# First quad's layer 0: one product or seven, and the order of what surrounds it

## The chip, the cores and the metric

The kernel runs on one core of a Trainium2 chip. The metric is the device time of one execution in microseconds (us); the median of the runs is compared. Engines are called by the profile's names where rows are read: PE is TensorE, PEld its weight loads, DVE is VectorE, ACT is ScalarE, POOL is GpSimd, SP is the queue of SyncE that issues most transfers.

## The reference

Sixteen batches of 1024 nodes with 128 features pass two layers over one 1024x1024 weighted adjacency matrix. All is float32.

```python
# layer 0
h = relu(layernorm(x))
x = x + adj @ (h @ W) + b
# layer 1: five gated steps
h = relu(layernorm(x))
for _ in range(5):
    m = adj @ h                                   # m_in and m_out are the same: one adj
    u = h @ U3.T + bu3
    z = sigmoid([m, m] @ W3.T + b3 + u)
    r = sigmoid([m, m] @ W4.T + b4 + u)
    hv = tanh([m, m] @ W5.T + b5 + (r * h) @ U5.T + bu5)
    h = (1 - z) * h + z * hv
out = x + h
```

## The kernel before

The batches are worked on in four quads of four. `adj @ h` (the aggregation) is the bulk of the work. A full two-level aggregation (`aggregate`, its matmuls are L502 of the profile) splits the adjacency matrix and the states into 2x2 blocks twice, and multiplies by seven products instead of eight at each level: 49 small products of two 128x128x256 matmuls each. It needs sums of the blocks on both sides. The sums of adjacency blocks ("right sums") are made once and stored to HBM (`rd`), from where they stream through a ring of 14 slots in SBUF; some are kept resident. The sums of states ("left sums") are made on VectorE in every aggregation (`big`, `little`). The opening of the program has to do, beside layer 0 of the first two quads, all that makes this possible.

The opening runs in this order. Quad 0's layer 0 is an aggregation without any trick (`aggregate_plainly`): for each half g of the nodes and each batch, eight matmuls of 128x128x512 over eight chunks c of the nodes, 64 in all. Quad 1's is `aggregate_by_seven`: one level of the seven products, each with four matmuls for i = 0 and four for i = 1 (two batches share a block row), 56 in all. Its right operands are the adjacency quarters R11, R21, R22 (raw tiles as loaded) and four sums T1 to T4 of quarters; its left operands are halves of the normed batches and four sums S1 to S4. Product p of `BIG = (1, 2, 6, 5, 7, 3, 4)` takes R11, R21, T2, T1, T3, R22, T4 in that order. T1 to T4 lie in ring slots, so the ring can be filled only when the products that read them are done. After each matmul group comes ScalarE's copy out of PSUM or VectorE's add from PSUM into the result tile `mT`. `po` multiplies a half of `mT` by the layer-0 weights (four 128x128x128 matmuls) and VectorE adds it to x (`xt`). Then follow layer 1's norm (`b0` to `b7`), and for quad 0 a store of the states in 32x32 squares (`park`, ft tiles), a load back (`sqt`) and VectorE's transposes of 32x32 squares (`transposing`, L699) that give the states with features on partitions.

The order is written out by hand. `pin` keeps program order on each engine, `put(k, piece)` hangs a piece of work behind place k, and `place(k)`, called after each product of an aggregation, emits what hangs there. So each engine runs its queue strictly in the written order, and an instruction that waits holds up all that stands behind it on its engine. Gate places have names such as "Az0" (pair A, second stage, first unit).

A layer norm is a `Norm`: `statistics` (VectorE, one `bn_stats` per chunk, L330), `scales` (VectorE aggregates and adds epsilon into `ve`, L339 and L341; POOL takes the inverse root `rstd`, L342), `shift` (VectorE's `nmr`, L347, which waits for POOL), `relu` (ScalarE, one activation per chunk, L360).

Loads are gated by tiny VectorE memsets: a memset of one element of the target tile makes the transfer wait until VectorE has come to that place. Before, all loads go out on SP in three such groups; x of batch 0 comes in three parts, adjacency tiles `raw[i][g]` (i: quarter rows, g: column half) in 512 KB pieces.

Step 0 of quad 0 is the first two-level aggregation, with quad 1's layer-1 norms beside it. Its left sums for the next products, the norm's statistics and the adds into the results all run on VectorE. After its 49 products come the gates. All later steps are the same in both kernels.

Of the kernel before, what the change touches and what calls it, by code (L numbers as in the profile page):

```python
# [96 lines left out]
def tile_two_gnn_layers(  # L97
# [50 lines left out]
    for n in (HALF, HALF, BLK):  # L148
        pin(nc.tensor.matmul(unread[:, 0:n], zeros[:, 0:P], zeros[:, 0:n], start=True, stop=True))
# [26 lines left out]
    def load_adj(i, g):  # L176
        parts = SB if (i, g) == (0, 0) else 1
        for k in range(parts):
            cs = bass.ts(k, SB // parts)
            dma(raw[i][g][:, cs], adjT[:, bass.ts(i, SB), bass.ts(g, HALF)][:, cs])  # L180

    xts = {0: load_x(0, parts=((0, 2), (2, CH), (CH, NC)))}
    xts.update({b: x_tile(b) for b in range(1, Q)})
    for i in range(2):
        load_adj(i, 0)

    early_x = {}

    def other_loads(k):
        if k == 0:
            pin(nc.vector.memset(xts[1][:, 0, 0:1], 0.0))
            load_x(1, xts[1])
            load_adj(2, 0)
        elif k == 1:
            pin(nc.vector.memset(raw[3][0][:, 0, 0:1], 0.0))
            load_adj(3, 0)
        else:
            pin(nc.vector.memset(xts[2][:, 0, 0:1], 0.0))  # L200
            for b in range(2, Q):
                load_x(b, xts[b])
            for i in range(NB):
                load_adj(i, 1)
            for b in range(Q, Q + 3):
                early(b)
            dma(gb, gbias.to_broadcast([P, D]))
            dma(w_sb, weights)
            dma(b_sb, biases)
# [31 lines left out]
    def right_sums():  # L241

        rooms = [flat(ring[:, 4 * k : 4 * k + 4]) for k in range(3)]
        count = [0]

        def big_sum(n):
            room = rooms[{1: 2, 2: 0, 3: 1, 4: 2}[n]]
            T[n] = [room[:, bass.ts(k, N)].rearrange("p (c n) -> p c n", c=SB) for k in range(2)]
            for k in range(2):
                R = {(a, b): raw[2 * (a - 1) + k][b - 1] for a in (1, 2) for b in (1, 2)}  # L250
                a, b = {
                    1: (R[1, 2], R[1, 1]),
                    2: (R[2, 2], T.get(1, [0, 0])[k]),
                    3: (R[2, 2], R[1, 2]),
                    4: (R[2, 1], T.get(2, [0, 0])[k]),
                }[n]
                sub(T[n][k], a, b)
# [10 lines left out]
        def small_sums(i, part):  # L268
# [3 lines left out]
            if part == 0:  # L272
                for p, block in ((1, r[1, 1]), (2, r[2, 1]), (3, r[2, 2])):
                    store_right((i, p), block)
# [12 lines left out]
        steps = [lambda n=n: big_sum(n) for n in (1, 2, 3)]  # L287
        steps += [lambda i=i, h=h: small_sums(i, h) for i in (3, 2, 0, 4, 1, 5) for h in range(2)]
        steps += [lambda: big_sum(4)]
        steps += [lambda h=h: small_sums(6, h) for h in range(2)]  # L290
        return steps
# [249 lines left out]
    def aggregate_plainly(hN, nm, place):  # L541

        k = 0
        for g in range(NH):
            for i in range(Q):
                bank = ps_g.tile([P, HALF], F32, tag="pg", name=f"pq_{nm}_{i}_{g}")
                for c in range(NC):
                    pin(
                        nc.tensor.matmul(
                            bank,  # L550
                            hN[i][:, c, :],
                            raw[c // SB][g][:, c % SB],
                            start=c == 0,
                            stop=c == NC - 1,
                        )
                    )
                    if c == CH - 1:
                        k += 1
                        place(k)
                pin(nc.scalar.copy(mT[:, i, bass.ts(g, HALF)], bank))  # L560
                k += 1
                place(k)

    def aggregate_by_seven(hN, nm, place):

        S = {}
        for n in (2, 1, 3):
            t = flip.tile([P, 2, CH, D], F32, tag="sq", name=f"S{n}_{nm}")
            S[n] = [t[:, i] for i in range(2)]
        S[4] = []  # L570
        for i in range(2):
            t = work.tile([P, HALF], F32, tag="hv", name=f"S4{i}_{nm}", bufs=3)
            S[4].append(t.rearrange("p (j d) -> p j d", j=CH))

# [3 lines left out]
        def left_sums(n):  # L578
            for i in range(2):
                op, x, y = {  # L580
                    1: (add, part(1, 0, i), part(1, 1, i)),
                    2: (sub, S[1][i], part(0, 0, i)),
                    3: (sub, part(0, 0, i), part(1, 0, i)),
                    4: (sub, part(0, 1, i), S[2][i]),
                }[n]
                op(S[n][i], x, y)
# [4 lines left out]
        left_sums(1)  # L591
        left_sums(2)
        banks, fifth = {}, {}
        k = 0
        for p in BIG:
            right = big_right(BIG.index(p)) if p in (1, 2, 3) else T[{5: 1, 6: 2, 7: 3, 4: 4}[p]]
            for i in range(2):
# [9 lines left out]
                name = {2: "b", 5: "c", 3: "c"}.get(p, "a")  # L607
# [5 lines left out]
                elif p == 5:  # L613
                    banks[name, i] = ps_g.tile([P, HALF], F32, tag="pg", name=f"{name}{i}_{nm}")
                bank = banks[name, i]
                for c in range(CH):
# [5 lines left out]
                            start=p in (1, 2, 5) and c == 0,  # L622
# [4 lines left out]
                if p == 2:  # L627
                    add(result(0, 0, i), bank, result(0, 0, i))
                elif p == 3:
                    add(result(0, 1, i), bank, result(0, 1, i))  # L630
                elif p == 5:
                    fifth[i] = work.tile([P, HALF], F32, tag="z", name=f"P5{i}_{nm}")
                    pin(nc.scalar.copy(fifth[i], bank))
                else:
                    o = {1: result(0, 0, i), 6: result(0, 1, i), 7: result(1, 1, i), 4: result(1, 0, i)}[p]
                    pin(nc.scalar.copy(o, bank))
                    if p == 7:
                        add(o, o, fifth[i])
                k += 1
                if k in (3, 4):  # L640
                    left_sums(k)
                place(k)

# [93 lines left out]
    def po(b, g):  # L737
# [12 lines left out]
        add(half, pt, half)  # L750
# [387 lines left out]
    one, two = Norm(xts[0], firsts[0][1], "a0"), Norm(xts[1], firsts[1][1], "a1")  # L1138
    parts = (range(2), range(2, CH), range(CH, NC))
    for k in range(2):  # L1140
        one.statistics(parts[k])
        one.scales(parts[k])
        if k == 0:
            other_loads(0)
    one.shift(parts[0])
    one.relu(parts[0])
    one.statistics(parts[2])
    one.scales(parts[2])
    other_loads(1)
    one.shift(parts[1])  # L1150
    one.relu(parts[1])
    one.shift(parts[2])
    one.relu(parts[2])
    two.statistics(range(CH))
    other_loads(2)
    two.statistics(range(CH, NC))
    two.scales(EVERY)
    two.shift(EVERY)
    two.relu(EVERY)
# [3 lines left out]
    def sums_at(k, n):  # L1163
        for _ in range(n):
            put(k, sums.pop(0))

    def norm_at(k, src, dst, nm, done=None, now=None):

        box = {}

        def begin():
            box["n"] = Norm(src(), dst, nm)
            box["n"].statistics(EVERY)
            box["n"].scales(EVERY)

        def rest():
            box["n"].shift(EVERY)
            box["n"].relu(EVERY)
            if done:
                done()  # L1180

        put(k, begin)
        if now is not None:
            sums_at(k, now)
        put(k + 1 if now is None else k, rest)

    norm_at(1, lambda: xts[2], firsts[2][1], "a2")
    norm_at(2, lambda: xts[3], firsts[3][1], "a3", now=0)
    sums_at(3, 1)
    for b, k in zip(range(Q, 2 * Q), (4, 5, 6, 8)):  # L1190
        done = (lambda: early(2 * Q - 1)) if b == Q else None
        norm_at(k, lambda b=b: early_x[b], seconds[b - Q][1], f"a{b}", done, 1)
    for b in range(Q):
        put(8 + b, lambda b=b: bias(b))
    for k in (7, *range(9, 16)):
        sums_at(k, 1)
    for b in range(Q):
        put(11 + b, lambda b=b: po(b, 0))
    put(15, lambda: po(0, 1))
    put(16, lambda: po(1, 1))  # L1200
    aggregate_plainly([s for s, _ in firsts], "a0", place)

    put(1, lambda: po(2, 1))
    put(2, lambda: po(3, 1))
# [6 lines left out]
    for (load, turn), k in zip(turns, (7, 8, 11, 12)):  # L1211
        put(k, load)
    for b in range(Q):
        norm_at(2 * b + 1, lambda b=b: xts[b], nat[:, b], f"b{b}", lambda b=b: first_done(b))
        put((3, 5, 7, 10)[b], lambda b=b: xts.update({Q + b: load_x(Q + b)}))
        put((6, 8, 10, 14)[b], lambda b=b: bias(Q + b))
    for k in (2, 4, 8, 9, 10):
# [81 lines left out]
```

## Time and profile before

| what | value |
|---|---|
| median of 3 runs | 1771.12 us (1770.43 to 1771.25) |
| the profiled execution | 1769.81 us, of which the span from first to last instruction is 1767.9 us |
| granted clock of TensorE | 1.00 in every stretch |
| first product of quad 0 | 5.90 us |
| first product of quad 1's layer 0 | 69.85 us |
| first product of step 0 | 126.85 us |
| first gate of step 0 | 170.08 us |

Times in the views are microseconds from the start of the span. A row of the order in time gives start, length, engine, line, operation, output and inputs, shapes, the number of instructions merged in it, and in brackets the idle time before it with what ended that. Every float32 matmul shows as two instructions, and the length of a row includes the drain of the last one, so the pitch is the distance between the starts of rows.

### The profile page before, as it was taken

What the parts mean: (1) busy time and instruction counts of PE and PEld (TensorE: products, weight loads), DVE (VectorE), ACT (ScalarE), POOL (GpSimd) and SP (SyncE); (2) the same over time, 40 slices, a digit from 0 to 9 for tenths busy, and PEclk for the clock granted to TensorE, in tenths of its full rate; (3) what the DMA queues carried; (4) which work ended last, traced back from release to release, by engine and by line L of the source; (5) the groups of instructions that cost most, each with busy time, mean ns of one, the idle gap of its engine ahead of it and who ended that gap; (6) DMA issues with size and microseconds to landing.
All of it is one profiled execution on the core that took longest, in us unless ns stands there. A gap on an engine that the chain in (4) does not pass through costs nothing.

```text
span 1767.9 us, 21431 instructions
## 1 busy us (share of the span) xinstructions
PE 1759.5 (100%) x6436; PEld 1201.0 (68%) x6436; DVE 1374.9 (78%) x2807; ACT 899.1 (51%) x1976; POOL 58.9 (3%) x41
## 2 busy tenths in 40 slices
PE   9999999999999999999999999999999999999999
PEld 4557667588585766858857667585766858667584
DVE  6778889777878687887687968777687777868687
ACT  5246555544555555554456554545455454545545
POOL 3101000000000000000000000000000000000000
PEclk9999999999999999999999999999999999999999
DMA  7499776678495956749749577594866749476684
GB/s 255 156 322 316 227 261 209 184 238 250 131 303 181 290 191 198 237 137 287 235 143 329 176 224 282 158 289 158 256 202 203 249 133 293 165 232 223 200 283 175
DMA packets 170258, 396.88 MB, mean 224 GB/s; under 512 B 18592, under 2 KB 88096, under 8 KB 170144
## 3 DMA queue, kind: packets, MB, share of 16 engines
q1 hardware_dynamic: 169712, 395.00, 69.6%
q8 instruction: 52, 0.85, 0.2%
q14 instruction: 62, 0.51, 0.1%
q10 hardware_dynamic: 432, 0.52, 0.1%
HBM read 314.44 MB, written 81.00 MB: 224 GB/s over the span
## 4 chain that ended last, share of the span: by engine, by line
PE 95%; DVE 2%; POOL 1%; DMA 1%; ACT 0%; issue 0%; DVEq 0%; POOLq 0%
PE a L502 27%; PE c L502 13%; PE b L502 7%; PE a_a L502 3%; PE pr_3B L806 2%; PE pr_2B L806 2%; PE pr_1B L806 2%; PE pr_0B L806 2%; PE pr_3A L806 2%; PE pr_2A L806 2%; PE pr_1A L806 2%; PE pr_0A L806 2%; PE pr_4B L806 2%; PE pr_4A L806 2%; PE a_a L618 2%; PE pv_1B L806 2%
## 5 line engine op out<-in xcount | busy, mean ns | idle before, releaser
L502 PE MATMUL a<-ring,big 128*128 128x256 f32 x1120 | 287.9, 379 | 0.3 <-ACT Z L521 0.3
L521 ACT COPY Z<-a 128x256 f32<-128x256 f32 x480 | 177.0, 371 | 193.0 <-PE a L502 192.9
L239 DVE TENSOR_TENSOR Z<-Z,taps 128x512 f32<-128x512 f32 (+1 forms) x264 | 144.6, 554 | 165.3 <-ACT taps L521 165.0
L502 PE MATMUL c<-ring,little 128*128 128x256 f32 x960 | 246.4, 379 | 0.0
L502 PEld LDWEIGHTS a<-ring,big 128*128 128x128 f32 x1120 | 212.2, 190 | 37.5 <-issue 8.1
L239 DVE TENSOR_TENSOR mT<-mT,Z 128x1024 f32<-128x1024 f32 x154 | 188.4, 1223 | 22.9 <-ACT Z L521 17.3
L502 PEld LDWEIGHTS c<-ring,little 128*128 128x128 f32 x960 | 182.2, 190 | 25.1 <-ACT taps L521 0.2
L521 ACT COPY taps<-c 128x256 f32<-128x256 f32 x280 | 103.6, 370 | 115.8 <-PE c L502 110.6
L502 PE MATMUL a<-resident,little 128*128 128x256 f32 x560 | 143.8, 379 | 0.0
L502 PE MATMUL b<-ring,big 128*128 128x256 f32 x560 | 143.7, 379 | 0.0
L502 PE MATMUL a<-ring,little 128*128 128x256 f32 x560 | 143.7, 379 | 0.0
L502 PEld LDWEIGHTS a<-resident,little 128*128 128x128 f32 x560 | 106.3, 190 | 14.7 <-ACT Z L521 0.3
L502 PEld LDWEIGHTS a<-ring,little 128*128 128x128 f32 x560 | 106.4, 190 | 14.5
L502 PEld LDWEIGHTS b<-ring,big 128*128 128x128 f32 x560 | 106.4, 190 | 14.5
L667 DVE STREAM_TRANSPOSE sq<-hT_all 128x512 f32<-128x512 f32 x152 | 98.6, 686 | 0.0
L239 DVE TENSOR_TENSOR little<-big 128x256 f32<-128x256 f32 x154 | 64.2, 417 | 21.5 <-ACT big L399 21.3
L399 ACT COPY big<-nat 128x512 f32<-128x512 f32 x132 | 80.7, 614 | 0.0
L521 ACT COPY taps<-b 128x256 f32<-128x256 f32 x140 | 52.0, 371 | 55.7 <-PE b L502 54.8
L236 DVE TENSOR_TENSOR little<-little,big 128x256 f32<-128x256 f32 x154 | 65.5, 425 | 6.7
L236 DVE TENSOR_TENSOR little<-big 128x256 f32<-128x256 f32 x154 | 64.4, 418 | 0.0
L236 DVE TENSOR_TENSOR little<-big,little 128x256 f32<-128x256 f32 x154 | 64.3, 418 | 0.0
L521 ACT COPY mT<-a 128x256 f32<-128x256 f32 x80 | 29.8, 372 | 48.3 <-PE a L502 48.3
(287 smaller groups left out, 2913.1 us busy)
## 6 DMA issues: line engine op xcount, KB each, us to landing
ring<-rd SPq DMA_DIRECT2D x440, 512.0 KB, 5.9
fn<-sq SPq DMA_DIRECT2D x76, 512.0 KB, 3.8
nat<-fn SPq DMA_DIRECT2D x256, 128.0 KB, 5.6
x1d<-xt SPq DMA_DIRECT2D x16, 512.0 KB, 5.2
sqt<-ft SPq DMA_DIRECT2D x16, 512.0 KB, 6.9
xt<-x1d SPq DMA_DIRECT2D x16, 512.0 KB, 7.4
xt<-in_x_dram SPq DMA_DIRECT2D x15, 512.0 KB, 5.5
ft<-hb SPq DMA_DIRECT2D x48, 128.0 KB, 5.2
```

Source lines behind the costliest of these rows:

```text
L236: pin(nc.vector.tensor_sub(o, a, b))
L239: pin(nc.vector.tensor_add(o, a, b))
L399: return [lambda i=i: pin(nc.scalar.copy(made_of(k, i), part(a, b, i))) for i in range(2)]
L502: nc.tensor.matmul(bank, l, right[:, c, :], start=opens and c == 0, stop=c == SB - 1, skip_group_check=True,)
L521: pin(nc.scalar.copy(to, bank))
L618: nc.tensor.matmul(bank, left[:, c, :], right[c // SB][:, c % SB], start=p in (1, 2, 5) and c == 0, stop=c == CH - 1, skip_group_check=True,)
L667: pin(nc.vector.transpose(squares_of_half(sq, g), transposed_half(hT, g)))
L806: nc.tensor.matmul(bank, w_sb[:, w, :], moving, start=start, stop=stop, skip_group_check=True)
```

## The change

Quad 0's layer 0 is done by `aggregate_by_seven` too, in the order (1, 2, 3, 5, 6, 7, 4), and `aggregate_plainly` is gone. Since product 3 now comes before product 5, it gets a PSUM bank of its own (`apart`, bank "d"), is copied out, and product 6's bank is added to it. The left sums S1 to S4 of quad 0 live in the state tile `hT_all[:, 0]`, which step 0 fills later; half of T4 lives there too.

Around it: the warm-up multiplication on zeros loses its third, narrower matmul. Loads come in four gated groups: the first half of x of batches 0 and 1 on SP with the first two adjacency tiles issued by ScalarE's queue; then the second halves and tile 2; then tile 3 and the batches 2 and 3; then the other adjacency halves; then the rest. The norms of the first quad run by half batches, the statistics of one half ahead of the `shift` of the half before it. The stores of plain adjacency blocks become pieces of their own (`store_blocks`), and VectorE's work in the opening is re-ordered: right sums, big sums in halves, delayed adds (`late`), `po` in two parts so that its add comes one place later (`po_at`). The layer-0 bias is no longer added on VectorE: ScalarE fills `xt` with the bias, and a load issued by POOL accumulates x into it (`with_bias`). Quad 0's transposes (their `sqt` loads on SP and VectorE's instructions) move from quad 1's layer 0 into step 0, at the places 15, 26, 49 and "Az0"; the weight sums move into step 0, place 5. The ring's first loads are issued inside quad 1's layer 0 (places 11 to 14). The relus of quad 1's layer-1 norms come one per place rather than two.

```diff
-    for n in (HALF, HALF, BLK):
+    for n in (HALF, HALF):
         pin(nc.tensor.matmul(unread[:, 0:n], zeros[:, 0:P], zeros[:, 0:n], start=True, stop=True))
...
+    xts = {b: x_tile(b) for b in range(Q)}
+    load_x(0, xts[0], ((0, 1), (1, 2), (2, CH)))
+    pin(nc.vector.memset(raw[0][0][:, 0, 0:1], 0.0))
+    load_adj(0, 0, nc.scalar)
+    load_x(1, xts[1], ((0, CH),))
+    load_adj(1, 0, nc.scalar)
...
     def other_loads(k):
         if k == 0:
+            mark(xts[0][:, CH, 0:1])
+            for b in range(2):
+                load_x(b, xts[b], ((CH, NC),))
             load_adj(2, 0)
         elif k == 1:
+            mark(raw[3][0][:, 0, 0:1])
             load_adj(3, 0)
+            for b in range(2, Q):
+                load_x(b, xts[b], ((0, CH), (CH, NC)))
+        elif k == 2:
+            mark(raw[2][1][:, 0, 0:1])
+            for i in (2, 3, 0, 1):
+                load_adj(i, 1)
         else:
+            mark(gb[:, 0:1])
+            dma(gb, gbias.to_broadcast([P, D]))
             for b in range(Q, Q + 3):
                 early(b)
...
+    def with_bias(b):
+        if b not in xts:
+            xts[b] = x_tile(b)
+        both = gb.unsqueeze(1).to_broadcast([P, NC, D])
+        pin(nc.scalar.copy(xts[b], both))
+        pin(nc.gpsimd.dma_start(out=xts[b], in_=by_slots(x[b]), accum_op=ALU.add))
...
-    aggregate_plainly([s for s, _ in firsts], "a0", place)
+    late = {(2, 0): 5, (2, 1): 5, (6, 0): 10, (6, 1): 10}
+    aggregate_by_seven([s for s, _ in firsts], S, "a0", place, (1, 2, 3, 5, 6, 7, 4), late)
...
+    for (load, turn), begun, done in zip(turns, (8, 17, 40, 46), (15, 26, 49, "Az0")):
+        put(begun, load)
+        put(done, turn)
...
-        for n in range(CH):
-            put(9 * k + 11 + n, lambda b=b, n=n: h1[b].relu(range(2 * n, 2 * n + 2)))
+        for n in range(NC):
+            put(9 * k + 10 + n, lambda b=b, n=n: h1[b].relu(range(n, n + 1)))
...
+    put(5, weight_sums)
     step(0, (41, 43, "Ar0", "Ar2"), early_places)
```

## The prediction

> **What bounds the kernel now.** I read the page first, then TensorE's waits, the stretches up to the first layer-1 gates, and the order of time there. The page:
>
> ```profile
> span 1767.9 us, 21431 instructions
> PE 1759.5 (100%) x6436; PEld 1201.0 (68%) x6436; DVE 1374.9 (78%) x2807; ACT 899.1 (51%) x1976; POOL 58.9 (3%) x41
> ...
> PE 95%; DVE 2%; POOL 1%; DMA 1%; ACT 0%; issue 0%; DVEq 0%; POOLq 0%
> ```
>
> TensorE (PE) is busy for 1759.5 of 1767.9 us and carries the chain. All that it ever waited for:
>
> ```profile
> PE unread L149 <- DVE zeros L146: 1.5, 1, 1.5
> PE po L741 <- DVE xt L239: 0.9, 1, 0.9
> PE pq_a L549 <- ACT nat L360: 0.7, 2, 0.4
> PE pq_a L549 <- DMA big<-in_adjT_dram: 0.7, 1, 0.7
> PE pf L932 <- DVE hT_all L239: 0.4, 1, 0.4
> PE a L502 <- ACT Z L521: 0.3, 1, 0.3
> ```
>
> So only fewer matmuls shorten this kernel, and a matmul saved counts only as far as no new wait stands in its place. The stretches (columns: from:to, length, busy us of PE, PEld, DVE, ACT, POOL, clock, DMA share, GB/s) are quad 0 before its first `po`, its rest, quad 1's layer 0, and step 0 up to its gates:
>
> ```profile
> 0.00:46.17 46.17, 43.30 (x95) 18.55 (x96) 31.52 (x163) 25.66 (x61) 15.82 (x15) 1.00 0.71 248
> 46.17:69.85 23.68, 22.78 (x89) 12.87 (x88) 16.58 (x24) 5.41 (x12) 0.57 (x1) 1.00 0.61 221
> 69.85:126.85 57.00, 57.00 (x194) 30.22 (x193) 41.86 (x127) 20.32 (x46) 6.63 (x4) 1.00 0.72 246
> 126.85:170.08 43.23, 42.96 (x199) 36.83 (x198) 38.67 (x128) 29.17 (x82) 6.87 (x4) 1.00 0.93 315
> ```
>
> VectorE has room until 126.85 and little after it (38.67 of 43.23). The rates come from the order of time (start, length, count; every fp32 matmul is two instructions):
>
> ```profile
> 1.45 4.64 PE L149 MATMUL unread<-zeros 128*128 128x512 f32 x6 [1.45 <-DVE zeros L146]
> 5.90 1.32 PE L549 MATMUL pq_a<-big,nat 128*128 128x512 f32 x2
> ...
> 78.51 7.03 PE L618 MATMUL b_a<-big,hT_all 128*128 128x512 f32 x16
> 85.38 7.03 PE L618 MATMUL a_a<-ring,S_a 128*128 128x512 f32 x16
> ```
>
> From 78.51 to 85.38 eight matmuls take 6.87 us: 0.859 each. A `po` of four narrow ones takes 0.89 (46.17 to 47.06). These and later numbers without a fence are rows of the same view.
>
> **The matmuls removed.** Quad 0 drops from 64 to 56 (the order of instructions confirms it): 8 x 0.859 = 6.87 us. Before, step 0 begins at 126.85 = 120 x 0.859 + 16 `po` x 0.89 (117.32) + 9.53 of start and stalls. After, the work is 110.44; the question is what stands in place of the 9.53. I walk the new order with these rows.
>
> **The start.** The first 64 KB of x land near 2.85 (128 KB did at 2.95). Statistics, aggregate, `ve`, `rstd`, `nmr` and relu for one chunk end at 4.85 (two chunks: 2.98 to 5.87 before). The warm-up loses two half-width instructions, and the first adjacency part comes from ACT's queue, issued while SP issues x; first product 5.05 (was 5.90). Chunk 1 follows at 6.0; chunk 2 waits for the second adjacency tile: 1.57 MB from 1.9 us at 258 to 292 GB/s (the 2 to 8 us rows) gives 8.0. Batch 1's half is normed from 9.3. Product 1 ends near 13.25: 1.33 of waits. The row of the zeros shows about 0.8 us per 512-wide instruction against 0.43 later, so the engine starts slow. The Trainium skill ("TensorE: Matmul & The Clock Gate", Part 1) says that about 3.4 us of sustained work are needed to open the clock, and that an idle gap as long closes it; a shorter warm-up speaks against the change, and by that rule alone a missed window would cost up to 1.7 us (an estimate; 1764.7 in the end). I book nothing, as product 1 is fed late anyway.
>
> **Products 2 and 3.** Product 2 (second halves, adjacency tiles 2 and 3) needs 2.62 to 3.14 MB, there by 12.8, and batch 1's second half, whose `nmr` stands on VectorE behind batch 2's statistics (landing 13.5, read by 14.8): relu from 15.1 against 16.7 needed, no wait; it ends at 20.1. Product 3 needs sums over all four batches, 4.19 MB of loads (15.6). A half batch costs VectorE 1.37 (5.08 to 6.36 in the trace, and an `nmr`), hence `nmr` of batch 3's halves at 19.2 and 20.9. The left sums are 128x256 steps of 0.42 at a pitch under 0.4 (the `little` rows), three per quarter: 20.6 and 22.1 for i=0; for i=1, behind the 1.15 us half of T1, 24.55 and 25.6. TensorE waits 0.5 before each i; product 3 ends at 28.0.
>
> **Products 5, 6, 7, 4.** Product 5 needs T1 (26.75): covered. After it VectorE runs T2 (to 29.05), two PSUM adds (30.3), batch 4's statistics (`ve` at 32.5), and then waits for POOL:
>
> ```profile
> 21.74 0.17 DVE L341 TENSOR_SCALAR ve_a<-mv_a 128x8 f32<-128x8 f32 x1
> 22.08 1.64 POOL L342 TENSOR_TENSOR rstd_a<-ve_a,mhalf 128x8 f32<-128x8 f32 x1 [2.67 <-ACT nat L360]
> 33.79 2.45 POOL L342 TENSOR_TENSOR rstd_a<-ve_a,mhalf 128x8 f32<-128x8 f32 x1 [2.67 <-DVE ve_a L341]
> ```
>
> The root takes 1.64 us alone and up to 2.45 beside VectorE sums. `nmr` at 34.75, batch 5's statistics and T3 to 40.0, product 6's add 40.8, the `po` add, half of T4, batch 6's statistics 44.8, `nmr` 47.1, and the add that completes result (0,1) at 47.75. `po(0,1)` stands on TensorE right after product 7's first half, at 46.9: it waits 0.85. Later adds are ahead of need (T4's second half 49.4 against 54.7). Quad 1 begins at 61.7 instead of 69.85. Its VectorE work, about 48 us by the same durations, lies under 57 of TensorE; its third and fourth left sums are done near 82 and 91 against 91 and 98, its residual sums and stores near 99, and six of the seven ring loads are issued there rather than from 115.33. So no wait: step 0 begins at 110.44 + 5.05 + 1.33 + 1.0 + 0.85 = 118.67, **8.2 us earlier**.
>
> **The bias.** Eight VectorE adds of 1.22 (9.8 us) go; eight ACT copies of 128x1024 (twice a 0.56 copy: 1.1) and eight accumulating loads on POOL come, four SP loads of x go. ACT does the first four from 24.3 to 28.7, ahead of copies that product 6's add needs only at 40; POOL issues the first at 25.4, and behind the four stands batch 4's `rstd`, wanted at 32.8. With t us of POOL per load, it is late by 25.4 + 4t - 32.8. The trace has no such load. The nearest POOL rows are 1.64 (late by nothing) and 2.45 (2.4 us late, passed on to `po(0,1)`); a gain beyond 0 is excluded, as TensorE doesn't wait for the old adds. I take 1.64, a row without contention, and keep 2.4 for the range. Landing is no issue by the plain loads (4 to 10.7 us; 15 are allowed). The skill's "SBUF — State Buffer" (two separate sides) warns of descriptors that GpSimd cannot write while VectorE holds the shared port: 0.62 us became 3.1. By that, 4t = 12.4 makes `rstd` 5.0 late, and the gain an estimated 3.2.
>
> **Step 0.** Moved in: four transposes (each a 512 KB load on SP and two 0.65 us VectorE instructions) and the weight sums (1.1 us). Before, one transpose of 1.29 already lay inside, with 1.25 of left sums that are now done earlier: net VectorE load 38.67 + 1.1 + 1.1 (third transpose, at the end) = about 41 of 43. The fourth lies in the gates, where VectorE is busy 6 of 10 us. On SP the first load stands behind three ring loads and goes out 5.7 us into the step, landing 6.9 later (the page's `sqt` median) at 12.6; VectorE reaches the transpose at 14.4. The left sums stay ahead of their products by 0.45 us at the tightest (fourth sum of the fourth big product) and 0.8 to 1.9 elsewhere. Before, step 0 lost 0.9 (43.23 against 49 x 0.864), after ScalarE ran relus in pairs between copies; they come singly now. I leave 0.9; bounds 0 and 2.4 (0.9 and a transpose's 1.29 unhidden, rounded up).
>
> Beyond, the order of instructions is the same, so the gain passes through: 1769.81 (this execution: 1767.9 span and 1.9 around it) - 8.2 = 1761.6. The median 1771.12 lies 1.3 above this execution: **1763.0**, rounded.
>
> **The rivals.** *Loads feed the norms late.* If the opening loads keep the first 6 us' 265 GB/s instead of reaching 350 to 400, batch 2 lands 1.7 us later, and products 3 and after slip by that: 1764.7. For it: smaller descriptors at the start. Against: 8 to 12 us already ran at 350 to 367.
> *VectorE falls behind* in step 0 and at `po(0,1)`: +1.5 and +2.4 (POOL at 2.45): 1766.9. For it: margins under 1 us in order; against: 10 us of its work is gone.
> *Slower: the accumulating loads hold POOL.* At t = 3.9 the lateness is 8.2 and the gain is gone; from t = 4.8 (11.8 late) the kernel is slower by over 0.2%; at t = 6 it is 16.6 late, 1779.6. Place: batch 4's `rstd`, in front of every VectorE step that product 7 needs. For it: no accumulating load in the trace. Against: POOL's longest instruction is 2.45.
> *The change isn't what it says*: excluded by the order, 56 matmuls and not 64.
>
> **How the numbers follow.** 0.2% (3.5 us) is about what a measurement of this kernel can tell from no change. Forecast 0.62; loads late 0.13; VectorE behind 0.13; POOL 0.12, two thirds of it past t = 4.8. Faster by over 0.2% (below 1767.6): 0.62 + 0.13 + over half of VectorE's case = 0.83; slower: 0.08; within: the rest, 0.09. The range: below, the waits of 1.0 and 0.85 and step 0's 0.9 not appearing, 1760.2; above, VectorE's case with the late loads (1.7), 1768.6.
>
> **What would show it.** Right: `aggregate_by_seven` starts near 5.05; TensorE waits of about 0.5 on the left sums near 20 and 24 and 0.85 at a `po` near 47; quad 1 at 61.7; step 0 at 118.7; gates 43 later; PE busy down by some 7. Wrong: a VectorE wait on POOL over 3 us near 33, waits on adjacency or x loads beyond 14 us, step 0 over 44.5, or steps after it that differ.

## The result, and the profile after

The changed kernel takes 1775.64 us (median of 8 runs, 1773.92 to 1777.46); the kernel before took 1771.11 beside it (8 runs, 1769.55 to 1772.91). The ratio is 1.0027, with a 95% interval of 1.0016 to 1.0038: slower by about 0.27%, where 8 us less were forecast. The execution profiled took 1773.92 us, the fastest of the eight, so what the trace shows of the loss is rather its lower end.

The page after, the lines that answer to those of before, and from its table of DMA queues (packets, MB, share of the time of 16 engines) one that is new, the accumulating loads:

```profile
span 1772.1 us, 21478 instructions
PE 1757.2 (99%) x6418; PEld 1198.8 (68%) x6418; DVE 1377.6 (78%) x2831; ACT 909.2 (51%) x1986; POOL 66.5 (4%) x53
...
q0 software_dynamic: 1152, 4.19, 1.3%
...
PE 91%; DVE 4%; DMA 3%; POOL 1%; issue 1%; SPq 0%; ACT 0%; DVEq 0%; POOLq 0%; ACTq 0%
```

TensorE has 18 recorded instructions fewer and 2.3 us less busy time, but it is no longer busy for the whole span, and in the chain that ended last VectorE went from 2% to 4% and DMA from 1% to 3%. What TensorE waited for (us in total, times, longest):

```profile
PE po L740 <- DVE mT L245: 3.9, 2, 3.5
PE pv_0B L808 <- DVE r_0B L821: 2.3, 1, 2.3
...
PE d_a L605 <- DVE hT_all L242: 1.2, 1, 1.2
PE a L516 <- ACT Z L535: 1.1, 1, 1.1
...
```

Two waits stand there that before had no like: 3.5 us for VectorE's `mT` at a `po`, and 2.3 us for `r_0B` at a gate. The third row shown is the left sum of quad 0's product 3 that the prediction had. The stretches (from:to, length, busy us of PE, PEld, DVE, ACT, POOL, clock, DMA share, GB/s): quad 0, quad 1's layer 0, step 0, and from step 0's first gate to the first gate of the next step:

```profile
0.00:62.65 62.65, 59.48 (x165) 27.89 (x166) 49.73 (x218) 35.85 (x79) 21.96 (x24) 1.00 0.79 254
62.65:125.04 62.39, 58.92 (x195) 31.01 (x194) 40.93 (x109) 24.33 (x50) 8.77 (x8) 0.97 0.83 253
125.04:167.51 42.47, 42.47 (x198) 37.15 (x197) 38.95 (x134) 30.71 (x82) 6.75 (x4) 1.00 0.88 302
167.51:250.82 83.31, 79.66 (x277) 52.59 (x276) 67.46 (x146) 43.01 (x96) 3.55 (x2) 0.98 0.85 269
```

Before, the four lasted 69.85, 57.00, 43.23 and 76.76. So quad 0 gained 7.20 and step 0 0.76; quad 1's layer 0 lost 5.39 (and its clock was 0.97 in the mean), and the last stretch lost 6.55 (0.98). That sums to +3.98, and it stays so to the end: each later first gate lies 3.9 to 4.0 us behind that of before.

**The first loss.** In the order of time, quad 1's layer 0 stops at 98.9 and goes on at 102.40 with a `po` that waits for VectorE's add of P5 into `mT` (L245, the last row); that add stands behind sums into tiles `t`, and these wait for the store of what the tile held before:

```profile
102.40 1.62 PE L740 MATMUL po<-w_sb,mT 128*128 128x128 f32 x8 [3.47 <-DVE mT L245]
103.81 3.12 PE L605 MATMUL c_a<-Z,hT_all 128*128 128x512 f32 x4
```

```profile
83.14 0.69 DVE L242 TENSOR_TENSOR t<-ring,resident 128x512 f32<-128x512 f32 x1
...
91.59 0.68 DVE L242 TENSOR_TENSOR resident<-Z 128x512 f32<-128x512 f32 x1
98.42 0.69 DVE L242 TENSOR_TENSOR t<-little,resident 128x512 f32<-128x512 f32 x1 [6.15 <-DMA rd<-t]
100.36 0.69 DVE L242 TENSOR_TENSOR t<-little,t 128x512 f32<-128x512 f32 x1 [1.25 <-DMA rd<-t]
...
101.57 0.68 DVE L245 TENSOR_TENSOR mT<-mT,P_a 128x512 f32<-128x512 f32 x1
```

VectorE idles 6.15 us ahead of one sum and 1.25 ahead of the next. There are eight tiles `t`, written in turn. The first one of this stretch was written at 83.14; SP's queue shows when its store went out:

```profile
85.49 4.12 SPq L129 DMA_DIRECT2D ft<-nat  x4
89.72 1.67 SPq L129 DMA_DIRECT2D x1d<-xt  x1
91.49 15.27 SPq L129 DMA_DIRECT2D rd<-t  x13
```

The 13 stores of `t` begin at 91.49, behind the slots of `ft` and `x1d`, and take 1.17 us each to issue. Meanwhile the DMA engines are full: from 86 to 104 us the packets of the two large queues take 53.3% and 51.1% of the engines' time (shown below).

**The second loss.** In step 0's gates VectorE waits twice for a `sqt` load:

```profile
173.75 1.30 DVE L691 STREAM_TRANSPOSE hT_all<-sqt 128x512 f32<-128x512 f32 x2 [4.08 <-DMA sqt<-ft]
...
184.28 1.30 DVE L691 STREAM_TRANSPOSE hT_all<-sqt 128x512 f32<-128x512 f32 x2 [6.07 <-DMA sqt<-ft]
...
197.90 1.85 DVE L821 TENSOR_TENSOR r_0B<-r_0B,hT_all 128x512 f32<-128x512 f32 x3
```

Both are the moved transposes, the third and the fourth. SP issued their loads at 164.79 and 180.28, each behind `ft` stores of layer-1 states (`hb`) that are further up its queue:

```profile
160.74 3.26 SPq L129 DMA_DIRECT2D ft<-hb  x4
164.09 0.60 SPq L129 DMA_DIRECT2D x1d<-xt  x1
164.79 0.66 SPq L129 DMA_DIRECT2D sqt<-ft  x1
...
175.01 3.91 SPq L129 DMA_DIRECT2D ft<-hb  x4
179.03 1.20 SPq L129 DMA_DIRECT2D x1d<-xt  x1
180.28 0.43 SPq L129 DMA_DIRECT2D sqt<-ft  x1
```

VectorE runs in order, so all that stands behind the transpose is late: the statistics of the next layer-0 norms, `hv_0A`, and then `r_0B` at 197.90, for which TensorE waits:

```profile
198.60 2.08 PE L808 MATMUL pv_0B<-r_0B,w_sb 128*128 128x512 f32 x2 [2.29 <-DVE r_0B L821]
```

In the next step TensorE waits another 1.06 us on ScalarE's copy at 221.37, a wait that is gone where the `sqt` loads are early (below); what held ScalarE up before that copy is not shown. Of the 6.55 us TensorE is idle for 3.65 (83.31 less 79.66 busy); some 1.6 more is what half clock cost behind the first wait (an estimate, half of the 3.3 us from 198.60 to its end, see the part on the clock), and the rest is spread over small delays.

### The profile page after: what moved, and what is told of

Same layout as the page of the kernel before. It is cut to its first block, busy times and chain, and to the rows that moved or that the text cites. A ratio compares the mean times of both kernels' runs of the same rounds, so it can differ in the third digit from the quotient of the medians.

```text
span 1772.1 us, 21478 instructions
## 1 busy us (share of the span) xinstructions
PE 1757.2 (99%) x6418; PEld 1198.8 (68%) x6418; DVE 1377.6 (78%) x2831; ACT 909.2 (51%) x1986; POOL 66.5 (4%) x53
## 4 chain that ended last, share of the span: by engine, by line
PE 91%; DVE 4%; DMA 3%; POOL 1%; issue 1%; SPq 0%; ACT 0%; DVEq 0%; POOLq 0%; ACTq 0%
PE a L516 27%; PE c L516 13%; PE b L516 7%; PE a_a L516 3%; PE pr_3B L808 2%; PE pr_1B L808 2%; PE pr_2B L808 2%; PE pr_2A L808 2%; PE pr_1A L808 2%; PE pr_3A L808 2%; PE pr_4A L808 2%; PE pr_0B L808 2%; PE pr_4B L808 2%; PE pr_0A L808 2%; PE pv_1B L808 2%; PE pv_3B L808 2%
## 5 line engine op out<-in xcount | busy, mean ns | idle before, releaser
L245 DVE TENSOR_TENSOR Z<-Z,taps 128x512 f32<-128x512 f32 (+1 forms) x264 | 144.6, 554 | 162.4 <-ACT taps L535 162.0
L245 DVE TENSOR_TENSOR mT<-mT,Z 128x1024 f32<-128x1024 f32 x154 | 188.4, 1224 | 22.6 <-ACT Z L535 16.9
L245 DVE TENSOR_TENSOR little<-big 128x256 f32<-128x256 f32 x154 | 64.5, 419 | 21.6 <-ACT big L413 21.4
```

The source lines that it names most:

```text
L245: pin(nc.vector.tensor_add(o, a, b))
```

## The experiments

The theory: the saved matmuls and the new opening are worth what was forecast; two late landings gave it back, the stores of `t` because the four accumulating loads of quad 1 crowd the DMA engines, and the third and fourth `sqt` loads because of their place on SP. The rivals: VectorE has too much work in either place, whatever lands when; it is the volume of transfers or SP's order and not the accumulation; the next step is slow for another reason.

All times are us; "quad 1" is the length of its layer 0, "gate to gate" the last stretch of the table above. The kernel before was run beside each set, median 1770.87 with the first four and 1770.38 with the last three.

| kernel | quad 0 | quad 1 | step 0 | gate to gate | span | median | ratio to before (95%) |
|---|---|---|---|---|---|---|---|
| before | 69.85 | 57.00 | 43.23 | 76.76 | 1767.9 | 1771.11 | |
| changed | 62.65 | 62.39 | 42.47 | 83.31 | 1772.1 | 1775.64 | 1.0027 (1.0016 to 1.0038) |
| transposes back | 62.45 | 64.87 | 42.31 | 76.77 | 1769.8 | 1768.94 | 0.9986 (0.9976 to 0.9995) |
| x overwrites | 62.49 | 57.27 | 42.48 | 81.42 | 1764.8 | 1767.32 | 0.9980 (0.9971 to 0.9989) |
| early `sqt` | 63.23 | 64.88 | 42.48 | 76.77 | 1768.7 | 1768.71 | 0.9991 (0.9980 to 1.0003) |
| bias back | 62.51 | 58.83 | 42.48 | 82.97 | 1768.4 | 1770.26 | 0.9996 (0.9986 to 1.0005) |
| plain loads, early `sqt` | 62.57 | 57.00 | 42.47 | 76.78 | 1761.5 | 1763.34 | 0.9958 (0.9947 to 0.9970) |
| overwrites, early `sqt` | 62.27 | 57.00 | 42.48 | 76.77 | 1760.6 | 1762.80 | 0.9955 (0.9943 to 0.9967) |
| more `t` tiles, early `sqt` | 63.26 | 58.55 | 42.47 | 76.78 | 1762.2 | 1763.39 | 0.9961 (0.9949 to 0.9974) |

**Transposes back in quad 1's layer 0.**

```diff
+    for (load, turn), k in zip(turns, (9, 10, 11, 12)):
+        put(k, load)
+    for (load, turn), k in zip(turns, (11, 12, 14)):
+        put(k, turn)
...
+    turns[-1][1]()
     for piece in early_0[10:]:
         piece()
-    for (load, turn), begun, done in zip(turns, (8, 17, 40, 46), (15, 26, 49, "Az0")):
-        put(begun, load)
-        put(done, turn)
```

> The changed kernel with one part undone: quad 0's four transposes go back into quad 1's layer 0 (loads at places 9 to 12, VectorE's turns at 11, 12, 14 and behind the last po). Theory (third and fourth sqt land late, and VectorE, which runs in order, waits for them in step 0's gates): the two waits of 4.08 and 6.07 us on sqt are gone, TensorE's 2.3 us wait on r_0B too, and from the first gate of step 0 to the first gate of the next step it takes 77 us as before the change (76.8) and not 83.3. That is worth 6.5 us, less what four more loads and 5.2 us of VectorE cost in quad 1's layer 0 (0 to 3): time 1769 to 1772.5. Rival (VectorE has too much to do around the gates, whatever lands when): the transposes are a quarter of the 10 us, so the distance stays above 81 us. Rival (the next step is slow for another reason, such as the relus that come singly): 83 us as it is.

Gate to gate it is 76.77, as before the change: the second loss is gone whole, and the relus that come singly have no part in it. Quad 1 is slower than in the changed kernel, 64.87; but with `sqt` early (below), where nothing in quad 1 differs from the changed kernel, it was 64.88 as well. So the first loss differs that much between profiled executions, and a price of the transposes can't be told from it (VectorE did wait 2.30 us for an `sqt` load at 109.47 here). The time, 1768.94, is just under the lower end expected.

**Overwriting loads.** One argument less; the queue, the bytes and the copies ahead stay. The kernel leaves out the layer-0 bias of quad 1, which the loads of x now overwrite.

```diff
-        pin(nc.gpsimd.dma_start(out=xts[b], in_=by_slots(x[b]), accum_op=ALU.add))
+        if b < Q:
+            pin(nc.gpsimd.dma_start(out=xts[b], in_=by_slots(x[b]), accum_op=ALU.add))
+        else:
+            pin(nc.gpsimd.dma_start(out=xts[b], in_=by_slots(x[b])))
```

> The changed kernel, but the four loads of x in quad 1's layer 0 overwrite instead of accumulating: same queue, same bytes, same places, same copies of the bias ahead of them (so the layer-0 bias is left out for quad 1's four batches). Theory (accumulating transfers keep the DMA engines busy longer and crowd the stores of the right sums, whose tiles VectorE waits for): the q0 share of the DMA engines drops, the stores of t land in under 5 us instead of 7.8, VectorE's 6.15 us wait at 98 falls below 3, TensorE's 3.5 us wait on mT at 102 is gone, and quad 1's layer 0 takes 57.5 to 59 us instead of 62.4; time 1768 to 1770. Rival (it is the sheer volume, or SP's order with ft and x1d ahead of the t stores): the same wait within 1 us, 62 us, 1772 to 1776.

Quad 1 takes 57.27 and TensorE's wait at the `po` is gone; the rival of volume or order would have left it. The transfers from 86 to 104 us, of the changed kernel and then of this one (queues: packets, MB, share of 16 engines; issues: count, KB, median us to landing):

```profile
DMA packets 2421, 5.02 MB, mean 279 GB/s; under 512 B 265, under 2 KB 1005, under 8 KB 2420
...
q1 hardware_dynamic: 1967, 3.35, 53.3%
q0 software_dynamic: 453, 1.66, 51.1%
...
rd<-t SPq DMA_DIRECT2D x10, 256.0 KB, 7.8
xt<-in_x_dram POOLq DMA_DIRECT2D x3, 512.0 KB, 8.3
```

```profile
DMA packets 3425, 6.61 MB, mean 367 GB/s; under 512 B 394, under 2 KB 1338, under 8 KB 3423
...
q1 hardware_dynamic: 2954, 4.93, 72.7%
q0 software_dynamic: 469, 1.66, 30.5%
...
rd<-t SPq DMA_DIRECT2D x13, 256.0 KB, 6.5
xt<-in_x_dram POOLq DMA_DIRECT2D x3, 512.0 KB, 6.4
```

The same 453 to 469 packets and 1.66 MB of x (queue q0) take 51.1% of the engines' 18 us when they accumulate and 30.5% when they overwrite: 9.2 and 5.5 us of all sixteen, or 180 and 302 GB/s. (Both windows are full, 104% and 103%.) The stores have what is freed: queue q1 moves 4.93 MB in the window and not 3.35, all together 367 GB/s and not 279; the 13 stores of `t` begin at 89.41 and take 0.95 us each to issue, and VectorE's wait falls from 6.15 to 3.91, with nothing of the 1.25 behind it. The last stretch is 81.42 here, 1.9 shorter than in the changed kernel, though the late `sqt` loads stay; so not all of the 8.3 us between the two medians is the first loss. Three numbers expected were off: the stores land in 6.5 us and not under 5, VectorE's wait is not under 3, and the time is 0.7 below the range; TensorE's wait went all the same.

**Early `sqt` loads.**

```diff
-    for (load, turn), begun, done in zip(turns, (8, 17, 40, 46), (15, 26, 49, "Az0")):
+    for (load, turn), begun, done in zip(turns, (8, 17, 33, 42), (15, 26, 49, "Az0")):
```

> The changed kernel, only that SP is given the third and fourth sqt loads at places 33 and 42 of step 0 instead of 40 and 46; VectorE's transposes stay where they are. Theory (late landing): both waits on sqt fall below 1 us, and from the first gate of step 0 to that of the next step it takes 77 to 78.5 us instead of 83.3; time 1767.5 to 1770.5. Rival (VectorE has too much work there): the waits go, but hv_0A and r_0B are still late and the distance is over 81 us. Rival (SP merely trades: nat loads for the next step come later by as much): a new wait on nat in the next step of 2 us or more.

Two places on one queue give back 6.5 us: SP issues the loads at 161.07 and 172.35 (step 0 begins 3.07 us later in this execution, so they are 6.8 and 11.0 us earlier by step 0's own time), and VectorE's third and fourth transposes, which stand where they stood, wait for nothing:

```profile
172.66 1.30 DVE L691 STREAM_TRANSPOSE hT_all<-sqt 128x512 f32<-128x512 f32 x2
...
179.77 1.29 DVE L691 STREAM_TRANSPOSE hT_all<-sqt 128x512 f32<-128x512 f32 x2
```

The instructions of VectorE are the same as in the changed kernel, so its load was not the cause; nor did a wait on `nat` take the place.

**The bias back on VectorE and SP**, for quad 1's batches:

```diff
-    for b, k in zip((Q + 2, Q + 3, Q, Q + 1), (4, 6, 8, 9)):
-        bias_at(k, b)
+    for b, k, at in zip((Q + 2, Q + 3, Q, Q + 1), (4, 6, 8, 9), (7, 9, 11, 12)):
+        put(k, lambda b=b: xts.update({b: load_x(b)}))
+        put(at, lambda b=b: bias(b))
```

> The changed kernel with the bias of quad 1's batches as before: plain loads of x on SP at the same places and VectorE's add of 1.2 us per batch, no copy on ScalarE and no accumulating load. Theory (accumulating loads): like the overwriting ones, TensorE's wait at 102 gone, quad 1's layer 0 in 57.5 to 59.5 us, 1768 to 1770.5. Rival (queue order on SP): now x also stands in SP's queue and waits there for the x1d stores, so the stores of t are as late as with the accumulating loads or later, 62 us or more and 1772 to 1777.

Quad 1 in 58.83: the theory's number, though 1.6 us of wait at the `po` are left. VectorE no longer waits for `rd` before it; it waits 1.14 and 1.98 us for x to land. The first of these loads went out at 84.18, ahead of the stores of `t`; the other three stand between them in SP's queue (at 92.70, 96.34 and 98.41), and the second wait, until 98.42, is for the one of 92.70. The rival's size was wrong, its mechanism is there in small.

**Both losses taken away, nothing left out.** Loads from POOL's queue without accumulation, early `sqt`:

```diff
-        bias_at(k, b)
+    def plain(b):
+        xts[b] = x_tile(b)
+        pin(nc.gpsimd.dma_start(out=xts[b], in_=by_slots(x[b])))
+
+    for b, k, at in zip((Q + 2, Q + 3, Q, Q + 1), (4, 6, 8, 9), (8, 10, 12, 13)):
+        put(k, lambda b=b: plain(b))
+        put(at, lambda b=b: bias(b))
...
-(8, 17, 40, 46)
+(8, 17, 33, 42)
```

> The changed kernel with both suspected losses taken away and nothing left out of the computation: the third and fourth sqt loads at places 33 and 42; quad 1's four x loads are plain loads issued by POOL at the same places, without the copy of the bias ahead of them, and VectorE adds the bias at places 8, 10, 12 and 13. Theory (the two late landings were the whole loss): TensorE waits under 2 us in all in quad 1's layer 0 (57 to 59 us), step 0 begins near 120 to 121.5, 43 us later come its gates, and the next step's first gate 77 us after those, near 240; the span is 3946.84-free arithmetic aside 5 to 7 us below the kernel before (1767.9): time 1763 to 1766, ratio to before 0.995 to 0.998. Rival (the 4.9 us of adds overload VectorE): a wait on mT or xt of 2 us or more in quad 1's layer 0, and 1767 to 1770.

(The words with 3946.84 in that text are a slip; no number stands behind them.) The four stretches:

```profile
0.00:62.57 62.57, 59.32 (x165) 27.63 (x165) 49.60 (x218) 35.86 (x79) 22.02 (x24) 1.00 0.80 254
62.57:119.57 57.00, 57.00 (x195) 30.22 (x193) 45.21 (x113) 20.46 (x46) 7.43 (x8) 1.00 0.81 277
119.57:162.04 42.47, 42.47 (x198) 37.16 (x197) 38.96 (x134) 30.48 (x82) 6.75 (x4) 1.00 0.90 322
162.04:238.82 76.78, 76.78 (x278) 52.35 (x276) 67.66 (x146) 43.93 (x96) 3.27 (x2) 1.00 0.86 280
```

TensorE waits for nothing in three of them, and VectorE's 4.9 us of adds cost nothing. The time is 1763.34, 0.42% below before (0.3 to 0.53%) and 0.7% below the changed kernel: this version beats both. At the end 1.18 us are lost to a ring load that is late at 1714.64, which before does not show.

**Both losses taken away, bias of quad 1 left out.** The two edits of the overwriting loads and the early `sqt` together.

> Both losses taken away with the bias left out for quad 1 (x overwrites, early sqt loads): the sum of the prediction without the two steps that failed. Theory: quad 1's layer 0 in 57.3 us and the distance between the two first gates 76.8 as each showed alone; first gate of step 0 near 162.3, next step's near 239, 7.8 us ahead of the kernel before (246.84): 1762 to 1764, ratio 0.9950 to 0.9962. Rival (the losses hide each other: an earlier step 0 finds its ring or sqt loads later): one of the two distances is over 1.5 us longer than alone, and 1765 to 1768.

57.00 and 76.77: each distance as short as alone or shorter, so neither loss hid the other. Step 0 begins at 119.27 and the next step's gate lies at 238.52, 8.32 ahead of before.

**More tiles for the right sums**, with the accumulating loads kept and `sqt` early:

```diff
-            t = work.tile([P, HALF], F32, tag="rz"[count[0] % 2], name=f"t_{key[0]}_{key[1]}")
+            n = count[0] % 11
+            if n < 3:
+                t = flat(taps)[:, bass.ts(n, HALF)]
+            else:
+                t = work.tile([P, HALF], F32, tag="rz"[n % 2], name=f"t_{key[0]}_{key[1]}")
```

> The accumulating loads stay; sqt loads early as in the run before; the right sums' tiles rotate over eleven rooms instead of eight (three more in taps, which is unused until step 0). Theory (VectorE waits for a tile whose store is late; the stores go out about 1.2 us apart): each wait is for a store three places earlier, so VectorE's waits on rd shrink by about 3.5 us, TensorE's wait on mT from 3.5 to 6.0 to 0 to 2.5, quad 1's layer 0 from 62.4 to 64.9 to 57.5 to 60.5; time 1763 to 1767. Rival (the accumulating loads hold TensorE up through something else, the x tiles or the ring): the wait stays over 3 us, 1768 to 1771.

With the loads as heavy as in the changed kernel (q0 again 1.3% of the span), three rooms more cut VectorE's waits on `rd` from 6.04, 3.85 and 1.15 (early `sqt` alone) to these two:

```profile
101.15 0.69 DVE L242 TENSOR_TENSOR t<-hT_all,t 128x512 f32<-128x512 f32 x1 [3.09 <-DMA rd<-t]
...
103.14 0.69 DVE L242 TENSOR_TENSOR t<-hT_all,t 128x512 f32<-128x512 f32 x1 [1.29 <-DMA rd<-t]
```

and TensorE's from 5.96 to 1.31. So the way from the accumulating loads to TensorE leads through the stores and the reuse of their tiles, and through nothing else of size.

## Why the prediction was wrong, step by step

**What held.** Eight matmuls less; the first product at 5.03 (5.05 predicted), product 1's end at 13.45 (13.25), product 2's at 20.6 (20.1). Product 1 came out by luck: the profile has none of the 1.33 us of waits there. Its first instructions start 0.93, 0.85 and 0.68 us apart and those after 7.49 us 0.43 apart, so a slow start took most of that time (the clock column shows 1.00 throughout). Product 3 waited 1.18 once rather than twice 0.5, because x of batch 2 landed at 15.05 and not 13.5, most of what the rival of late loads had (1.7); `po(0,1)` waited 0.40 for 0.85. Quad 1 began at 62.65, 0.95 later than the walk gave. Step 0 even ran without the 0.9 of loss that was left in it (42.47): VectorE behind in step 0, a rival, was not seen before the gates. With the two losses taken away, or the first nearly so, the forecast of 1763.0 is met within 0.4 us by all three kernels (1763.34, 1762.80, 1763.39). That it is so close is in part luck, since quad 0's 0.95 too much and step 0's 0.76 too little all but cancel; what carries the miss is two terms put at nothing.

**The step that failed first** is the bias, and with it "So no wait: step 0 begins at 110.44 + ... = 118.67". "Landing is no issue by the plain loads" asked whether x would be there in time for its `po`; it was (8.3 us in quad 1's window, 11.5 in quad 0's; 15 allowed). It did not ask what eight loads of an unseen kind do to the transfers beside them. Quad 1's VectorE work "lies under 57 of TensorE" by its busy time, 40.93 of 62.39, but a tile that waits for its store is not in a sum of busy time. The term put at 0 was 5.39: 3.47 of waiting and 1.9 behind it, most of it slow clock; with early `sqt`, where the stretch is the same, it was 7.9.

**The second** is the moved transposes: only the first load's landing was walked (predicted out 5.7 us into the step; it went out 5.74 in). "The fourth lies in the gates, where VectorE is busy 6 of 10 us" looked at VectorE's room and not at SP's queue, where each of the two stands behind four `ft` stores and an `x1d`. That term, also put at 0, was 6.55, and because the wait holds VectorE in front of the chain r, hv, it passed to TensorE with the delay of the gates and was felt into the next step: "the order of instructions is the same, so the gain passes through" was wrong there.

**The slower rival** had the right sign and the wrong place. For POOL, held by the accumulating loads, to undo the gain would have taken 3.9 us for each; four took 3.77 in all, beside VectorE's big sums, and the root then waited for VectorE, not VectorE for the loads:

```profile
26.53 3.77 POOL L734 DMA_DIRECT2D xt<-in_x_dram  x4 [5.04 <-ACT xt L733]
33.90 1.96 POOL L356 TENSOR_TENSOR rstd_a<-ve_a,mhalf 128x8 f32<-128x8 f32 x1 [3.60 <-DVE ve_a L355]
```

VectorE's wait for the root was 1.55 us, not over 3. The Trainium skill's warning ("SBUF — State Buffer", two separate sides) of descriptors that GpSimd cannot write while VectorE holds the shared port did not show: 0.94 per issue, not 3.1. The page gives it for VectorE's two-port modes, a `tensor_copy` in its measurement, and not for sums of two tensors; beside these four issues VectorE ran such sums (`TENSOR_TENSOR`, from 26.76). What the loads cost, they cost on the DMA engines. There the Trainium skill has the rule: "DMA: Bandwidth & Descriptors" says under "Issuing engines are not separate DMA queues" that transfers of all issuing engines share the same 16 engines, and under "Rules for kernel authors" that an accumulating transfer reads its destination and writes it later. The two measured rates, 180 and 302 GB/s for the same bytes, agree with both; no run here shows whether the second read is the reason.

**The clock.** The shorter warm-up shows in product 1's slow start (instructions 0.43 apart from 7.49 us, before from about 6.6), but product 1's second half had to wait for batch 1's relu (9.37 to 9.86) in any case, so little of the 1.7 us that the rule would have allowed can have reached the end. The clock came back in two places that the prediction had without a wait. In 1 us stretches (columns as above, clock third from the end) after the 2.29 us wait for `r_0B` in the changed kernel, and after one of 2.27 us at the same instruction with the bias back:

```profile
198.00:199.00 1.00, 0.40 (x1) 0.40 (x2) 1.00 (x2) 0.00 (x0) 0.00 (x0) 0.73 0.22 90
199.00:200.00 1.00, 1.00 (x2) 0.44 (x2) 1.00 (x3) 0.00 (x0) 0.00 (x0) 0.50 1.03 377
200.00:201.00 1.00, 1.00 (x2) 0.34 (x1) 0.97 (x3) 0.28 (x1) 0.00 (x0) 0.50 0.97 315
201.00:202.00 1.00, 1.00 (x2) 0.34 (x1) 1.00 (x6) 0.40 (x1) 0.00 (x0) 0.57 0.66 266
202.00:203.00 1.00, 1.00 (x4) 0.49 (x3) 1.00 (x3) 0.00 (x0) 0.00 (x0) 1.00 0.03 8
```

```profile
194.00:195.00 1.00, 0.43 (x1) 0.30 (x2) 1.00 (x2) 0.00 (x0) 0.00 (x0) 1.00 0.56 229
195.00:196.00 1.00, 1.00 (x4) 0.41 (x3) 1.00 (x3) 0.26 (x1) 0.00 (x0) 1.00 1.08 389
```

Once the clock fell to half, for 3.4 us by the shares of these rows (0.54 + 1 + 1 + 0.86), and the two instructions at 198.60 took 2.08 in place of 1.13; the other time it stayed. Part 1 of the Trainium skill's "TensorE: Matmul & The Clock Gate" lets an idle window of about 3.4 us close the clock and calls the window free-running. The first gap was shorter than that and closed it, so here the measurement stands against the figure; the halving and the 3.4 us until it opened agree. Waits of 1.60, 1.86 and 1.31 us left the clock at 1.00; those of 3.47, 5.33 and 5.96 closed it, the last two for 6.8 us. The phase can tell the near twins apart: in the changed kernel the clock falls at 102.88 and 198.46, 28 steps of 3.41 us apart, so its changes seem to lie on a grid, as a free-running window would have it. On that grid the gap of 2.29 put 2.15 us of idling into one step; with the bias back, counted from the clock's fall at the end of the trace (1767.74), no step had over about 1.9. This is an estimate; no run shifted a gap along the grid.

What stays open: why the first loss goes from 5.4 to 7.9 us between executions of the same instructions. The spread of single executions is wide there too (1765.44 to 1774.29 with accumulating loads and early `sqt`, against 1761.58 to 1765.66 with plain loads), but no run tells what sets it.

## What to carry to other kernels

A step that is freed from one engine's list by giving it to a transfer has to be priced for the transfers beside it, and for each tile whose reuse waits on a store: busy time on the engine doesn't hold that wait, the order on the issuing queue does. When a load and its use are moved, walk every load through the queue that issues it, the last as well as the first; what stands ahead of it there decides when it lands, and an engine that runs in order passes its lateness to everything behind. Where TensorE is the bound, price a new gap of over 2 us at its length and, if the clock closes, at 1.6 to 2.4 us more, which is half of the time that TensorE here ran on at half clock (3.3 to 4.7 us after the gap).

## What the runs showed of the hardware

Accumulating loads took 1.7 times the engine time of plain ones for the same bytes (9.2 against 5.5 us of sixteen engines for 1.66 MB), and POOL's issue of one took 0.86 to 1.05 us against 0.53 to 0.62. A gap of 2.29 us closed TensorE's clock once, and one of 2.27 did not.
